# Gate and up products of a gated MLP as seven block products, with the order of work from a table

## The chip, the cores and the metric

The kernel runs on one core of one Trainium2 chip. The metric is the device time of one execution in microseconds (us); lower is better. A core has five engines that run side by side: TensorE (PE, the matrix engine; its weight loads are shown as PEld), VectorE (DVE), ScalarE (ACT), GpSimd (POOL) and SyncE (SP, which here only issues DMAs). Each engine works through its own queue in order and waits for the others through semaphores. SBUF is the working memory, PSUM the memory in which TensorE accumulates, in eight banks of 128 partitions x 512 float32.

## What is computed

Two layers over x of 2 x 1024 tokens with 256 channels: a mixture of gated MLPs, of which the two best of eight experts and one shared expert count for each batch row, and a linear layer with a LoRA mix.

```python
def mlp(x, gate_w, up_w, down_w):          # 256 -> 1024 -> 256
    g = einsum('bsh,hi->bsi', x, gate_w)
    u = einsum('bsh,hi->bsi', x, up_w)
    return einsum('bsi,ih->bsh', gelu(g, approximate=True) * u, down_w)

w, sel = top_k(softmax(cond), 2); w = w / w.sum()
x = x + sum(w_e * mlp(x, expert_e) for e in sel) + mlp(x, shared)
x = x + x @ W_base.T + b_base + 2 * lora(x, cond, As, Bs)
```

Everything is float32. The kernel splits each float32 operand v exactly into two parts, hi (v rounded to 12 significant bits, as float32r) and lo = v - hi, and forms a product as hi*hi + lo*hi + hi*lo: three matmuls for each float32 product.

## The kernel before

All is transposed: channels on the partitions, tokens on the free axis. A block is 512 tokens (T = 2 blocks for each of B = 2 batch rows), which is one PSUM bank. The 1024 hidden units of an expert are NI = 8 chunks of 128. `chunks` (L147 ff.) lists batch row, expert (s = 0 is the shared one) and chunk: 2 x 3 x 8 = 48 chunks. The main loop steps over chunks, and inside over the two token blocks: 96 steps.

A step (`gate_up`) forms the gate product g and the up product u. Each has two 128-row halves of the 256 channels, so each is 2 x 3 matmuls of 512 columns into one PSUM bank (`product`, L236). ScalarE applies gelu to g (L256), VectorE multiplies by u and, for an expert, by its weight (L259, L261), ScalarE makes the hi part (L263) and VectorE the lo part (L266). Two steps later (`DEPTH`) `down` multiplies these by the chunk's down weights, six matmuls (L282), which accumulate over all chunks of a batch row in the two banks of y of that block. So a step is 18 matmuls of 128x512.

Weights: a piece is two chunks, 768 KB. SP loads the shared ones; POOL gathers those of chosen experts by an indirect DMA (L169), with an index found by the router. Four raw buffers, loaded some seven chunks ahead. VectorE splits each chunk, 768 columns for gate, up and down together, in two instructions (L179, L183), which are put between a step's own instructions through the list `todo`.

At the start, 32 matmuls of constants run on PE while the first loads arrive; the first piece is loaded in column parts so that the first product can begin early. The LoRA matrix of a batch row (`weff_split`, `weff_mix`, `weff_add`) is made during the first chunks, in pieces spread over eight chunks of steps. The last layer (`lora`) of the first batch row runs inside the second row's first steps; at the end its stores are halved.

The order is that in which the Python code writes the instructions down: a last loop chains each engine's instructions in that order.

Of the kernel before, what the change touches and what calls it, by code (L numbers as in the profile page):

```python
"""x + top-2 mixture of gated MLPs with a shared expert, then + a linear layer with mixed LoRA.

Everything runs transposed: channels on partitions, tokens on the free axis, so that
no product needs a transpose on the chip. The host only permutes axes of the inputs.

One router row serves a whole batch row of 1024 tokens. The router runs on the chip; the
weights of the two chosen experts of each batch row are gathered by indirect DMAs with the
indices found there (the other experts enter the reference's sum with a weight of exactly 0).

The LoRA mix of a batch row is one matrix for all of its tokens, so  # L10
    W_eff[b] = W_base + 2 * sum_e cond[b, e] * Bs[e] @ As[e]
is formed once per batch row and the second layer is x + x @ W_eff[b].T + b_base.

Products: each float32 operand v is split exactly into float32r parts, hi = v rounded to 12
significant bits and lo = v - hi, which has at most 12. A product of two operands is then
three single-pass products, hi*hi + lo*hi + hi*lo, accumulated in float32; what lo*lo would
add is below half a unit in the last place of a float32 product.

Weights are outermost: each chunk of 128 hidden units is loaded and split once per batch row
and used for both of its token blocks.  # L20
"""
# [16 lines left out]
TB = 512      # tokens of a block: one PSUM bank of float32  # L38
TOP_K = 2
SCALING = 2.0  # LoRA's alpha / r  # L40
PIECE = 2     # chunks of 128 hidden units in one weight load
DEPTH = 2     # steps that a block's second product runs behind its first
WARM = 32     # products of constants that raise the tensor engine's clock while the first loads run
AHEAD = 3     # chunks that are split ahead of their use
LOAD_AHEAD = 7  # chunks that are loaded ahead of their use
# [3 lines left out]
def moe_then_lora(ctx: ExitStack, tc: tile.TileContext, xT, cond, skill, shared, wbT, bias,  # L49
# [5 lines left out]
    CW = 3 * C                      # weights of a chunk of 128 hidden units, per partition  # L55
    PW = PIECE * CW
    NPC = skill.shape[0] // (E * P)  # pieces of an expert
    NI = NPC * PIECE
    R = P // E
    S = NT // B  # L60
    T = S // TB

    const = ctx.enter_context(tc.tile_pool(name="const", bufs=1))
    rawp = ctx.enter_context(tc.tile_pool(name="rawp", bufs=4))
    wp = ctx.enter_context(tc.tile_pool(name="wp", bufs=7))
    xs = ctx.enter_context(tc.tile_pool(name="xs", bufs=4))
    xr = ctx.enter_context(tc.tile_pool(name="xr", bufs=2))
    work = ctx.enter_context(tc.tile_pool(name="work", bufs=4))
    resp = ctx.enter_context(tc.tile_pool(name="resp", bufs=4))
    post = ctx.enter_context(tc.tile_pool(name="post", bufs=2))  # L70
    ps_gu = ctx.enter_context(tc.tile_pool(name="ps_gu", bufs=2, space=bass.MemoryType.PSUM))
    ps_y = ctx.enter_context(tc.tile_pool(name="ps_y", bufs=2, space=bass.MemoryType.PSUM))

    def xview(n0):
        return xT[:, n0:n0 + TB].rearrange("(c p) n -> p c n", p=P)

    logits = const.tile([P, B, E], F32, name="logits")
    nc.gpsimd.dma_start(out=logits, in_=bass.AP(cond.tensor, 0, [[0, P], [E, B], [1, E]]))

# [1 line left out]
    row = const.tile([P, NPC], I32, name="row")  # L81
    nc.gpsimd.iota(row, pattern=[[1, NPC]], base=0, channel_multiplier=NPC)
    top = const.tile([P, B, 8], F32, name="top")
    gap = const.tile([P, B], F32, name="gap")
    ex = const.tile([P, B], F32, name="ex")
    sel = const.tile([P, B, 8], U32, name="sel")
    at = const.tile([P, B, TOP_K, NPC], I32, name="at")
    den = const.tile([P, B], F32, name="den")
    gate_w = const.tile([P, TOP_K, B], F32, name="gate_w")

    def router_max():
        for b in range(B):
            nc.vector.max(out=top[:, b, :], in_=logits[:, b, :])

    def router_exp():
        nc.vector.tensor_tensor(gap, top[:, :, 1], top[:, :, 0], ALU.subtract)
        nc.scalar.activation(ex, gap, AF.Exp)

    def router_index():
        for b in range(B):  # L100
            nc.vector.max_index(out=sel[:, b, :], in_max=top[:, b, :], in_values=logits[:, b, :])
        for b in range(B):
            nc.vector.scalar_tensor_tensor(
                at[:, b], sel[:, b, 0:TOP_K].unsqueeze(2).to_broadcast([P, TOP_K, NPC]), float(P * NPC),
                row.unsqueeze(1).to_broadcast([P, TOP_K, NPC]), ALU.mult, ALU.add,
            )

    def router_weights():
# [282 lines left out]
    while late:  # L391
        down(*late.pop(0))
# [59 lines left out]
```

## Time and profile before

| what | value |
|---|---|
| time, median of 3 runs | 420.66 us (420.38 to 420.96) |
| profiled execution, span on the core | 418.5 us, granted TensorE clock 0.995 |
| TensorE matmul busy | 411.1 us, 1832 instructions |
| VectorE / ScalarE / GpSimd busy | 226.4 / 126.3 / 25.5 us |
| 128x512 matmuls in the gate and up products / in the down products | 1152 / 576 |
| first matmul of the kernel's own / gapless from about | 5.2 us / 9.2 us |
| last result on VectorE ends / span ends | 415.0 / 418.5 us |

The span is the time from the first to the last instruction of one execution that the hardware profiler recorded. It is about 2 us below the median of the runs; sums are made against the span and then moved by this difference. "Busy" of PE is the union of overlapping matmuls; a group's row gives the length of one instruction from start to end, which is not the distance between two of them.

A line of a timeline has: start in us, duration in us, engine, source line, operation, output <- inputs, shapes, and in brackets the idle time before it with the one it waited for.

### The profile page before, as it was taken

What the parts mean: (1) busy time and instruction counts of PE and PEld (TensorE: products, weight loads), DVE (VectorE), ACT (ScalarE), POOL (GpSimd) and SP (SyncE); (2) the same over time, 40 slices, a digit from 0 to 9 for tenths busy, and PEclk for the clock granted to TensorE, in tenths of its full rate; (3) what the DMA queues carried; (4) which work ended last, traced back from release to release, by engine and by line L of the source; (5) the groups of instructions that cost most, each with busy time, mean ns of one, the idle gap of its engine ahead of it and who ended that gap; (6) DMA issues with size and microseconds to landing.
All of it is one profiled execution on the core that took longest, in us unless ns stands there. A gap on an engine that the chain in (4) does not pass through costs nothing.

```text
span 418.5 us, 4602 instructions
## 1 busy us (share of the span) xinstructions
PE 411.1 (98%) x1832; PEld 339.8 (81%) x1832; DVE 226.4 (54%) x351; ACT 126.3 (30%) x207; POOL 25.5 (6%) x27
## 2 busy tenths in 40 slices
PE   6999999999999999999999999999999999999996
PEld 5888888888888888888888888888888888888884
DVE  3956665454545445754695454544545454554346
ACT  3522223322222233222242222223322222333231
POOL 2201011011010000000030101001011000000000
PEclk8999999999999999999999999999999999999999
DMA  7752021120220322031027322022021000000003
GB/s 211 252 191 76 2 75 31 46 76 5 72 75 2 125 75 76 1 105 72 0 75 209 72 73 76 0 78 75 0 78 62 13 2 0 2 0 0 2 1 100
DMA packets 8837, 25.99 MB, mean 62 GB/s; under 512 B 1504, under 2 KB 2928, under 8 KB 8816
## 3 DMA queue, kind: packets, MB, share of 16 engines
q1 hardware_dynamic: 6480, 13.11, 9.7%
q0 software_dynamic: 2336, 12.59, 9.4%
q8 instruction: 14, 0.23, 0.2%
q14 instruction: 7, 0.06, 0.0%
HBM read 23.60 MB, written 2.10 MB: 61 GB/s over the span
## 4 chain that ended last, share of the span: by engine, by line
PE 95%; DMA 1%; DVE 1%; ACT 1%; issue 1%; SPq 0%; DVEq 0%
PE u L236 31%; PE g L236 31%; PE y L282 30%; PE o L236 2%; DMA x_raw<-in_xT 1%; ACT xa_hi L294 0%; PE wps L236 0%; DVE xa L293 0%; DVE xa_lo L297 0%; DVE act L261 0%; DVE x_lo L138 0%; ACT act_hi L263 0%; DVE res L311 0%; DVE x_hi L137 0%; SPq L152 0%
## 5 line engine op out<-in xcount | busy, mean ns | idle before, releaser
L261 DVE SCALAR_TENSOR_TENSOR act<-ge,gate_w,u 128x512 f32<-128x512 f32 x64 | 48.0, 749 | 118.7 <-PE u L236 118.5
L263 ACT CAST act_hi<-act 128x512 fp32r<-128x512 f32 x96 | 59.8, 622 | 146.4 <-DVE act L261 99.2
L256 ACT ACTIVATE ge<-g 128x512 f32<-128x512 f32 x96 | 57.5, 599 | 125.3 <-PE g L236 125.3
L236 PE MATMUL g<-x_hi,w_hi 128*128 128x512 f32 x192 | 75.0, 391 | 2.2 <-DVE x_hi L137 1.4
L236 PE MATMUL g<-x_lo,w_hi 128*128 128x512 f32 x192 | 75.1, 391 | 0.2 <-DVE x_lo L138 0.2
L236 PE MATMUL u<-x_hi,w_hi 128*128 128x512 f32 x192 | 75.2, 391 | 0.0
L236 PE MATMUL g<-x_hi,w_lo 128*128 128x512 f32 x192 | 75.0, 391 | 0.1
L236 PE MATMUL u<-x_lo,w_hi 128*128 128x512 f32 x192 | 75.1, 391 | 0.0
L236 PE MATMUL u<-x_hi,w_lo 128*128 128x512 f32 x192 | 74.9, 390 | 0.0
L266 DVE TENSOR_TENSOR act_lo<-act,act_hi 128x512 fp32r<-128x512 f32 x96 | 66.1, 688 | 12.7 <-ACT act_hi L263 12.5
L282 PE MATMUL y<-act_hi,w_hi 128*128 128x512 f32 x192 | 59.1, 389 | 0.0
L282 PE MATMUL y<-act_hi,w_lo 128*128 128x512 f32 x192 | 59.1, 389 | 0.0
L282 PE MATMUL y<-act_lo,w_hi 128*128 128x512 f32 x192 | 59.1, 389 | 0.0
L259 DVE TENSOR_TENSOR act<-ge,u 128x512 f32<-128x512 f32 x32 | 22.0, 687 | 46.9 <-PE u L236 46.8
L183 DVE TENSOR_TENSOR w_lo<-w_raw,w_hi 128x768 fp32r<-128x768 f32 x47 | 44.7, 951 | 0.0
L236 PEld LDWEIGHTS g<-x_hi,w_hi 128*128 128x128 f32 x192 | 36.1, 188 | 10.2 <-DVE x_hi L137 1.7
L236 PEld LDWEIGHTS g<-x_hi,w_lo 128*128 128x128 f32 x192 | 36.2, 189 | 7.9 <-POOL w_lo L159 0.5
L236 PEld LDWEIGHTS u<-x_hi,w_hi 128*128 128x128 f32 x192 | 36.3, 189 | 7.7
L236 PEld LDWEIGHTS g<-x_lo,w_hi 128*128 128x128 f32 x192 | 36.2, 188 | 7.8 <-DVE x_lo L138 0.5
L236 PEld LDWEIGHTS u<-x_lo,w_hi 128*128 128x128 f32 x192 | 36.3, 189 | 7.6
L236 PEld LDWEIGHTS u<-x_hi,w_lo 128*128 128x128 f32 x192 | 36.3, 189 | 7.6
L282 PEld LDWEIGHTS y<-act_hi,w_hi 128*128 128x128 f32 x192 | 36.0, 188 | 7.5
(53 smaller groups left out, 209.8 us busy)
## 6 DMA issues: line engine op xcount, KB each, us to landing
w_raw<-in_shared SPq DMA_DIRECT2D x7, 768.0 KB, 7.1
x_raw<-in_xT SPq DMA_DIRECT2D x8, 256.0 KB, 5.1
x_res<-in_xT SPq DMA_DIRECT2D x4, 512.0 KB, 5.6
outT<-res SPq DMA_DIRECT2D x6, 256.0 KB, 2.8
outT<-res SPq DMA_DIRECT2D x4, 128.0 KB, 2.5
w_raw<-in_shared SPq DMA_DIRECT2D x3, 128.0 KB, 4.7
w_raw<-in_shared SPq DMA_DIRECT2D x1, 384.0 KB, 6.7
wbT_sb<-in_wbT SPq DMA_DIRECT2D x1, 256.0 KB
```

What stands on the lines that cost most here:

```text
L183: nc.vector.tensor_tensor(lo, raw_w[j], hi.bitcast(F32), ALU.subtract)
L236: nc.tensor.matmul(ps, lhsT=l, rhs=r, start=(n == 0), stop=(n == len(parts) - 1))
L256: nc.scalar.activation(ge, g, AF.Gelu_apprx_tanh)
L259: nc.vector.tensor_tensor(act, ge, u, ALU.mult)
L261: nc.vector.scalar_tensor_tensor(act, ge, gate_w[:, s - 1, b:b + 1], u, ALU.mult, ALU.mult)
L263: nc.scalar.copy(hi, act)
L266: nc.vector.tensor_tensor(lo, act, hi.bitcast(F32), ALU.subtract)
L282: nc.tensor.matmul(y[:, c, :], lhsT=d[:, o:o + P], rhs=a, start=first and n == 0, stop=last and n == 2,)
```

## The change

The kernel is rewritten around a *group*: two chunks of hidden units and both token blocks of a batch row, for one expert. With 24 groups, gate (h = 0) and up (h = 1) of a group are each a product of a 2x2 block matrix (two chunks by two halves of the channels, A11 to A22) and a 2x2 block matrix of x (two halves of the channels by two token blocks). This is done by Strassen's scheme in Winograd's form: seven block products P1 to P7, of three matmuls each, instead of eight. For that,

- four sums of weight blocks are made on POOL for each group (`weight_sum`), of 128x256, gate and up side by side; and hi and lo parts of three plain blocks (`wa`, 128x768), four sums (`ws`, 128x1024) and the down weights (`wd`, 128x512);
- four sums of x blocks are made once for each batch row (`x_sum`), and hi and lo of seven operands instead of four;
- results are sums over several products. Some are accumulated in a PSUM bank: bank "a" of a half takes P1, then P6 on top, then P7, then P4; bank "d" takes P2, then P5 and P3. Between them ScalarE copies the partial sum of bank "a" to SBUF (`keep`, three for each half), and VectorE adds a kept part to bank "d" (`add_part`, three for each half).

Names: ij = (0,0), (1,1), (1,0), (0,1) are the four results of a group (chunk i, token block j). keep r1, u2 and u3 are the copies after P1, P6 and P7; add_part (0,0), (1,1), (0,1) are the sums with them, and (1,0) is what bank "a" holds after P4.

Every call is entered in a list with a time (`at(t, f, ...)`), a slot number: 22 slots for a group (`LEN`), each slot of PE being one block product or half a down product. The list is sorted by time and executed; each engine's queue follows from it. Tiles come from rings of fixed length (`Ring`): two raw weight buffers instead of four.

```diff
-WARM = 32     # products of constants that raise the tensor engine's clock while the first loads run
-AHEAD = 3     # chunks that are split ahead of their use
-LOAD_AHEAD = 7  # chunks that are loaded ahead of their use
+WARM = 32
+LEN = 22
...
+    raw_ring = Ring(sb, 2, [P, PW], F32, "w_raw")
+    wa_ring = Ring(sb, 2, [P, 2, 3 * G2], F32R, "wa")
+    sf = const([P, 4 * G2], F32, "sf")
+    ws_ring = Ring(sb, 2, [P, 2, 4 * G2], F32R, "ws")
+    bank = {(m, h): pp.tile([P, TB], F32, name=f"ps_{m}{'gu'[h]}", tag=f"{m}{h}")
+            for m in "ad" for h in (0, 1)}
...
+    def weight_sum(g, i, eng):
+        a, b, op = (
+            (raw_block(g, "A21"), raw_block(g, "A22"), ALU.add),
+            (ssum(0), raw_block(g, "A11"), ALU.subtract),
+            (raw_block(g, "A11"), raw_block(g, "A21"), ALU.subtract),
+            (raw_block(g, "A12"), ssum(1), ALU.subtract),
+        )[i]
+        eng.tensor_tensor(ssum(i), a, b, op)
...
+    def product(ps, terms, start=True):
+        parts = [p for (lh, ll), (rh, rl) in terms for p in ((lh, rh), (lh, rl), (ll, rh))]
+        for n, (l, r) in enumerate(parts):
+            nc.tensor.matmul(ps, lhsT=l, rhs=r, start=(start and n == 0), stop=(n == len(parts) - 1),
+                             skip_group_check=True)
...
+    def keep(m, h):
+        nc.scalar.copy(part[m, h], bank["a", h])
+
+    def add_part(g, h, ij, m):
+        sums[g, h, ij] = sum_ring[h].next()
+        nc.vector.tensor_tensor(sums[g, h, ij], bank["d", h], part[m, h], ALU.add)
...
+    for i in range(4):
+        at(-6.6 + i / 100, weight_sum, 0, i, G)
+    at(-6, split_ws, 0, hi_of, A)
+    at(-5.8, split_wa, 0, 2, 3, hi_of, A)
+    at(-5, x_sum, 0, 3, V)
+    at(-5, x_sum, 0, 1, V)
+    at(-5, x_sum, 0, 2, V)
+    at(-4.9, split_x, 0, "P6", hi_of, A)
+    at(-4.8, split_x, 0, "P6", lo_of, V)
+    at(-4.7, split_ws, 0, lo_of, V)
...
+    at(-3.9, split_x, 0, "P4", hi_of, A)
+    at(-3.8, split_x, 0, "P4", lo_of, V)
+    at(9.1, router)
+    at(-1, split_wd, 0, hi_of, A)
+    at(-0.9, split_wd, 0, lo_of, G)
+    for b in range(B):
+        at(7 + b, weff_split, b)
+        at(9.5 + b, weff_mix, b, y[b][0])
+        at(10.7 + b, weff_add, b, y[b][0])
+
+    ACT_AT = {(0, 0): 5.6, (1, 1): 15.6, (1, 0): 18.5, (0, 1): 21.5}
+    LO_AT = {(0, 0): 7.8, (1, 1): 18.0, (1, 0): 20.8, (0, 1): 23.5}
+    GE_AT = {(0, 0): 3.5, (1, 1): 14.4, (1, 0): 16.4, (0, 1): 18.4}
+    HI_AT = {(0, 0): 6.7, (1, 1): 16.8, (1, 0): 19.6, (0, 1): 22.6}
+    DOWN_AT = {(0, 0): (14, 19), (1, 1): (20, 21), (1, 0): (26, 31), (0, 1): (32, 35)}
+    PE_AT = (
+        (0, 0, "P1", "a", True), (1, 0, "P2", "d", True), (2, 1, "P1", "a", True), (3, 1, "P2", "d", True),
+        (5, 0, "P6", "a", False), (6, 0, "P5", "d", True), (7, 1, "P6", "a", False), (8, 1, "P5", "d", True),
+        (11, 0, "P7", "a", False), (12, 1, "P7", "a", False),
+        (15, 0, "P4", "a", False), (16, 0, "P3", "d", False),
+        (17, 1, "P4", "a", False), (18, 1, "P3", "d", False),
+    )
+    for g, (b, s, q) in enumerate(groups):
+        t0 = g * LEN
+        if g + 2 < NG:
+            at(t0 + 1.2, load_w, g + 2)
...
+        for t, m, h in ((1.3, "r1", 0), (3.3, "r1", 1), (6.3, "u2", 0), (8.3, "u2", 1),
+                        (12.3, "u3", 0), (13.3, "u3", 1)):
+            at(t0 + t, keep, m, h)
+        for t, h, ij, m in ((2.4, 0, (0, 0), "r1"), (4.4, 1, (0, 0), "r1"), (13.4, 0, (1, 1), "u3"),
+                            (14.3, 1, (1, 1), "u3"), (17.3, 0, (0, 1), "u2"), (19.5, 1, (0, 1), "u2")):
+            at(t0 + t, add_part, g, h, ij, m)
...
+        if g + 1 < NG:
+            n = g + 1
+            for i in range(4):
+                at(t0 + 1.5 + i, weight_sum, n, i, G)
+            at(t0 + 9.0, split_ws, n, hi_of, A)
+            at(t0 + 9.6, split_ws, n, lo_of, V)
+            at(t0 + 10.4, split_wa, n, 0, 3, hi_of, A)
+            at(t0 + 11, split_wa, n, 0, 3, lo_of, G)
+            at(t0 + 20.4, split_wd, n, hi_of, A)
+            at(t0 + 20.8, split_wd, n, lo_of, G)
```

In these calls A is ScalarE, V VectorE and G POOL. `weff_split`, `weff_mix`, `weff_add` and the whole router now stand in the first group (slots 7 to 11.7). For the second batch row, `x_sum` (POOL) and the splits of x are entered in groups 10 and 11, the residual adds `finish_y` of the first row in group 12, and the first row's last layer at the very end, between the last down products. There stores are of a whole 128x512 block.

## The prediction

> **What bounds the kernel now.** I read the page's busy time, then the chain that ended last, the groups, and timelines of start and middle.
>
> ```profile
> span 418.5 us, 4602 instructions
> ...
> PE 411.1 (98%) x1832; PEld 339.8 (81%) x1832; DVE 226.4 (54%) x351; ACT 126.3 (30%) x207; POOL 25.5 (6%) x27
> ...
> PE 95%; DMA 1%; DVE 1%; ACT 1%; issue 1%; SPq 0%; DVEq 0%
> ```
>
> TensorE (PE) is busy 98% of the span and is 95% of the chain; other engines end no wait that matters. Removing a matmul is worth its pitch, as long as the others keep up.
>
> ```profile
> L263 ACT CAST act_hi<-act 128x512 fp32r<-128x512 f32 x96 | 59.8, 622 | 146.4 <-DVE act L261 99.2
> L256 ACT ACTIVATE ge<-g 128x512 f32<-128x512 f32 x96 | 57.5, 599 | 125.3 <-PE g L236 125.3
> L236 PE MATMUL g<-x_hi,w_hi 128*128 128x512 f32 x192 | 75.0, 391 | 2.2 <-DVE x_hi L137 1.4
> ...
> L266 DVE TENSOR_TENSOR act_lo<-act,act_hi 128x512 fp32r<-128x512 f32 x96 | 66.1, 688 | 12.7 <-ACT act_hi L263 12.5
> ...
> L183 DVE TENSOR_TENSOR w_lo<-w_raw,w_hi 128x768 fp32r<-128x768 f32 x47 | 44.7, 951 | 0.0
> ```
>
> These durations price the new side work. Matmuls overlap: 391 ns is a latency; the chain shows six in 1.36 us, a pitch of 0.2267.
>
> ```profile
> 100.77 0.75 DVE L261 SCALAR_TENSOR_TENSOR act<-ge,gate_w,u 128x512 f32<-128x512 f32 x1 [1.95 <-PE u L236]
> ...
> 101.43 0.95 DVE L183 TENSOR_TENSOR w_lo<-w_raw,w_hi 128x768 fp32r<-128x768 f32 x1
> 101.55 0.62 ACT L263 CAST act_hi<-act 128x512 fp32r<-128x512 f32 x1 [1.56 <-DVE act L261]
> ...
> 102.30 0.68 DVE L266 TENSOR_TENSOR act_lo<-act,act_hi 128x512 fp32r<-128x512 f32 x1
> ```
>
> VectorE starts its next instruction 0.09 us before the last ends (0.66 for 0.75). So a 512-wide tensor_tensor occupies 0.60. At 17.00 and 17.53 two ScalarE instructions start 0.53 apart. An engine hands over to another in 0.03 to 0.06; a reader of PE starts 0.49 after the last matmul's start (398.11, then 398.60).
>
> ```profile
> 8.65 0.79 PE L236 MATMUL g<-x_lo,w_hi 128*128 128x512 f32 x1 [0.16 <-DVE x_lo L138]
> ...
> 10.37 0.75 POOL L159 TENSOR_TENSOR w_lo<-w_raw,w_hi 128x256 fp32r<-128x256 f32 x1 [1.07 <-ACT w_hi L158]
> ...
> 10.52 0.63 PE L236 MATMUL u<-x_hi,w_lo 128*128 128x512 f32 x1
> ...
> 10.56 1.10 DVE L138 TENSOR_TENSOR x_lo<-x_raw,x_hi 128x512 fp32r<-128x512 f32 x1
> ...
> 11.96 0.39 PE L236 MATMUL g<-x_hi,w_hi 128*128 128x512 f32 x1
> ```
>
> Two things of the start: x_lo beside a GpSimd (POOL) subtraction takes 1.10 instead of 0.69 and ends 0.54 after POOL does; and after PE's first waits the matmuls run at a pitch of 0.43 until 11.4. At 11.96, 12 matmuls (2.7 us) are done: the start costs 9.2.
>
> **The Trainium skill.** "SBUF — State Buffer", Who interferes with whom: a VectorE instruction with two SBUF inputs and a GpSimd instruction that reads SBUF exclude each other for their whole length. The x_lo above agrees. The indirect gather's POOL row (102.65, 1.22 us) beside act_lo at 0.68 shows no such effect. "TensorE: Matmul & The Clock Gate", What's actually happening: full clock returns after some 3.4 us of work; the slow pitch above agrees. "PSUM — Partial Sum Buffer" (The four PSUM rules) allows a synchronised read of a partial sum; no run here shows its price, so I price it as other PSUM reads.
>
> **Part 1, matmuls.** A group is two chunks and both token blocks. Before: 48 gate/up and 24 down matmuls. After: 14 block products of three, 42, and the same 24. 24 groups save 144 x 0.2267 = 32.6 us. PE's work was 391.7 (1728 matmuls) + 11.0 (last layer) + 1.4 (LoRA mix) = 404.1; it becomes 359.1 + 10.9 + 1.4 = 371.4. Every old matmul already loads its own weights at this pitch, so I leave the pitch.
>
> **Part 2, side work per group** (PE 66 x 0.2267 = 14.96 us). ScalarE: 15 instructions of 512 (six keeps, four gelus, four act_hi, one wd) x 0.53, a 1024 and a 768 (estimates from 405 ns at 256 and 622 at 512: 1.0 and 0.8): 9.8. VectorE: 13 to 14 of 512, x 0.60 to 0.66, and ws_lo of 1024, 1.14: 9.7. POOL: four sums at 0.73, lo of 768 (1.84, extrapolated) and of 512 (1.29): 6.1, plus 1.22 where it gathers. All fit singly. Sizes not in the trace: 1024 on VectorE is the 768 row plus one more step of 951 - 688 = 263 ns, 1.21 long; a ScalarE copy out of PSUM lies between gelu's 599 (from PSUM) and act_hi's 622 (a copy from SBUF), so nothing is gained or lost there; add_part is xa<-y,x_res again, 680 ns.
>
> Weight loads: the raw ring has two tiles instead of four. A load is issued behind POOL's last reading of the group before and is first read by the next weight sums, one group later. Landing took 7.1 us (shared) and 5.3 (gather), so about 8 us of cover is left; it costs nothing unless a transfer takes twice as long. The gather itself stands ahead of the four sums in POOL's queue: its 1.22 us is in the walk below.
>
> Order and latency: a slot is three matmuls, 0.68 us; slot k ends at 0.68(k+1), readers start 0.27 later. Walking one group in its queue orders without the lock: keep u3 g reads slot 11 at 8.43 and ends at 9.04 (P4 needs it at 10.14); add_part(1,1) g then ends at 9.76 (P3 needs it at 10.82); act_hi(1,1) ends at 12.30 (needed 13.54); times_up(0,1) ends at 15.82, act_hi(0,1) at 16.5, and keep r1 behind it in ScalarE's queue at 17.0, where the next P6 needs it at 18.3. Each is over 1 us early: PE stays the bound.
>
> With the lock, at two places: wd_lo becomes ready just as act_lo(1,0) ends and may go ahead of times_up(0,1), +1.1 us on the way to the next act_hi(0,1); and the four sums alternate with act_lo(0,1), times_up(0,0) and act_lo(0,0), so ws_hi, queued ahead of keep u3 on ScalarE, starts some 1 us later. Without POOL VectorE's loop (issue 12.0 plus waiting for ws_hi 0.9) closes in 12.9. Adding both places and wa_lo, POOL first each time, I get 15.4 in the 16 groups in which POOL also gathers, about 14.7 in the others. So 0 to 0.44 a group; I take 0.2 x 16 = 3.2.
>
> **Part 3, start.** Loads: the first four DMAs carry what the first ones did, so P1 and P2 finish at about 12.5 (slow pitch included). Then PE needs P6, whose bank waits for keep r1 g. On ScalarE that stands behind ws_hi, A22's hi, five x hi and wd_hi; on VectorE add_part stands behind three x sums, five x lo, ws_lo and a fourth sum. x11 lands at about 10.2 (before, its last x cast starts at 10.11); three x sums alternate with POOL's four sums: ws_hi at 13.3; P6 lo ends at 16.0, ws_lo at 17.2, three lo at 19.0, fourth sum 19.7, P4 hi 20.4, wd_hi 20.9, keep r1 at 21.4. Four slots are done then: PE idle for 9 us.
> Then VectorE carries the first group's extra work ahead of add_part(1,1): LoRA splits (2.0 + 1.2 us), router (1.6), ws_lo (1.1), two weff_add of three instructions (3.7; rows 683, 452, 693 ns), besides two adds, times_up, act_lo (2.5), a ScalarE table load for gelu (1.28; exp between two gelus adds two more of them behind this one, beside VectorE's router work) and 0 to 2 us of POOL's lock. That is 13.4 to 15.4: from 21.4 to about 35 or 37. P3 g starts 0.7 later, with 12 slots (8.2) and the mix (1.4) done: 26 to 28 lost. With the uncertain landings and P6's wait, 23 to 29; I take 26 (before 9.2). The router's gather index is needed only in group 2.
>
> **Part 4, batch change and tail.** Groups 10 to 12 add six x lo and four residual adds to VectorE (6.0 us), seven casts to ScalarE, and five 1.29 us instructions to POOL, of which two stand ahead of group 11's weight sums. Their slack is about 2 us a group: 1 to 6, I take 3. The tail stores 256 KB last instead of 128 KB; its VectorE order (finish_y, lo, store) leaves PE fed by the (0,1) second layer. 5.0 before, 4.6 to 5.2 after: 4.8.
>
> **Sum**: 371.4 + 26 + 3.2 + 3 + 4.8 = 408.4 against the profile's 418.5. The median shown, 420.66, is 2.2 above that span: 410.6, so 411.
>
> **Rivals.** A, this sum with its bounds: 402 to 421.
> B, the lock costs nothing: VectorE's instructions follow one another before POOL gets in, and the start takes 23. For: the walk's slacks of 1 us; against: the x_lo of 1.10. 371.4 + 23 + 0 + 1 + 4.8 = 400.2, time 402.
> C, slower: the lock becomes the loop. If every SBUF-reading POOL instruction holds up VectorE, its loop is 9.7 + 6.1 = 15.8 us a group, 0.8 over PE's: 23 x 0.8 = 18.4 in place of the 3.2, 423.6, time 426. It decides from (418.5 - 371.4 - 26 - 3 - 4.8)/23 = 0.58 us a group, a period of 15.5. For: VectorE works much of each group with two SBUF inputs; against: six adds read PSUM and are free of the lock, and half of POOL's work can fall beside them.
> D, the matmuls don't get fewer or take a longer pitch: the instruction order shows 42 and 24 a group. Under 0.02, counted in C.
>
> **How the numbers follow.** A 0.50, B 0.25, C 0.25. Forecast 411. The range 401 to 425 holds A, B and C's lower half. 0.2% (0.8 us) is what a measurement can tell from no change. Faster: A 0.46 + B 0.25 + C 0.03 = 0.74; same 0.02 + 0.02 = 0.04; slower 0.02 + 0.20 = 0.22.
>
> **What would show it.** The middle slices of the page: PE at 9 everywhere and a group each 14.96 us is B; 15.0 to 15.4 with waits of PE on keep, ws_hi's followers or add_part is A; 15.5 or more, with act_lo, times_up or ws_lo well over 0.69, 0.75 and 1.21, is C. The start: P6 at about 21 and P3 at 34 to 38 is right; P3 before 30 makes me wrong by that much. If PSUM reads between products take much over 0.62, or the pitch leaves 0.2267, Parts 1 and 2 fall.

## The result, and the profile after

| | before | after |
|---|---|---|
| median of the runs | 420.52 us (420.28 to 420.96) | 416.45 us (415.53 to 416.95) |
| ratio of the times, 95% interval | | 0.9893 (0.9875 to 0.9911) |
| span of the profiled execution | 418.5 us | 414.7 us |

The change makes the kernel 4.1 us faster; 9.7 us were forecast. The page of the changed kernel shows, in the lines that answer to those shown of before (span; busy time of each engine; in tenths, the busy share of PE in 40 slices of the span, and the clock granted to it; the chain that ended last):

```profile
span 414.7 us, 4765 instructions
...
PE 388.6 (94%) x1676; PEld 312.5 (75%) x1676; DVE 330.6 (80%) x425; ACT 260.0 (63%) x435; POOL 207.5 (50%) x177
...
PE   7287999999999999999889999999999999999993
...
PEclk8678999999999999999999999999999999999998
...
PE 68%; DVE 11%; issue 8%; POOL 5%; ACT 4%; DMA 3%; SPq 1%; DVEq 0%; POOLq 0%
```

PE is busy for 22.5 us less, but it was busy 98% of the span and is now busy 94%; only 68% of the chain are its own, where it was 95%. The slices say where: the first four (a slice is 10.4 us) read 7287, and the 20th and 21st read 88, in the middle of the span, where one batch row follows the other. Between these two places and behind the second PE is full (90% or more in each slice). The groups show what the others paid (instructions of one kind; busy us, mean ns of one, then idle time before them):

```profile
L151 DVE TENSOR_TENSOR acts<-act,acts 128x512 fp32r<-128x512 f32 x96 | 78.4, 816 | 34.1 <-ACT acts L148 31.6
...
L279 DVE SCALAR_TENSOR_TENSOR act<-ge,gate_w,c_u 128x512 f32<-128x512 f32 x48 | 58.4, 1217 | 4.0 <-DVE c_u L264 0.5
L190 POOL TENSOR_TENSOR sf<-w_raw 128x256 f32<-128x256 f32 x48 | 51.8, 1080 | 1.5 <-DMA w_raw<-in_shared 1.0
```

times_up with both inputs in SBUF takes 1217 ns where it took 749 with one of them in PSUM, act_lo 816 instead of 688. The form alone is not the reason, since the same times_up takes 739 ns at its shortest, where no POOL instruction runs beside it: the exclusion between VectorE and POOL is there. In an ordinary group it costs next to nothing, as the next view shows. Its rows are whole groups, each from the start of its P1 to that of the next (us; then busy us and number of instructions of PE, PEld, DVE, ACT and POOL, granted clock, DMA share, GB/s): group 2, then groups 10, 11, 12 and 13.

```profile
55.37:70.33 14.96, 14.96 (x67) 12.33 (x66) 12.09 (x16) 10.25 (x17) 8.40 (x8) 1.00 0.18 54
175.55:191.02 15.47, 15.25 (x68) 12.31 (x66) 13.06 (x17) 10.37 (x18) 9.04 (x7) 1.00 0.14 52
191.02:209.97 18.95, 16.50 (x68) 11.93 (x66) 17.32 (x20) 12.31 (x23) 12.47 (x10) 1.00 0.11 42
209.97:227.12 17.15, 15.81 (x68) 12.15 (x66) 14.76 (x20) 10.56 (x18) 8.49 (x7) 1.00 0.31 108
227.12:243.41 16.29, 15.55 (x68) 12.23 (x67) 12.82 (x18) 10.92 (x19) 7.21 (x7) 1.00 0.33 113
```

A group without side work of the second row takes 14.96 to 15.07 us (group 22 alone 15.48), where 66 matmuls at 0.2267 are 14.96; before, 72 took 16.32. Groups 10 to 13 take 0.5, 4.0, 2.2 and 1.3 us more, 8.0 in all. So the span adds up as 371.4 (PE's work) + 26.8 (start) + 1.6 (groups 1 to 9 and 14 to 22, of which 0.5 in group 22) + 8.0 (groups 10 to 13) + 7.0 (tail) = 414.8, the span but for rounding. The start's 26.8 is where group 1 begins, 40.40, less the 12.24 of the 18 slots done by then and the 1.4 of the LoRA mix; the tail's 7.0 is the span less the start of group 23 (379.12), one group (14.96) and the 13.6 of work that then remains (four half down products, 2.7, and the last layer, 10.9).

Where group 11 loses its 4.0 us is seen in its timeline (start, duration, engine, line, output <- inputs; in brackets the idle time before it and whom it waited for):

```profile
193.08 1.75 POOL L224 TENSOR_TENSOR xr<-xr,xr 128x512 f32<-128x512 f32 x1
...
194.87 0.96 PE L247 MATMUL ps_ag<-x,ws 128*128 128x512 f32 x3 [0.29 <-ACT r_g L258]
194.91 1.62 POOL L226 TENSOR_TENSOR xr<-xr,xr 128x512 f32<-128x512 f32 x1
...
196.03 0.97 PE L247 MATMUL ps_dg<-x,ws 128*128 128x512 f32 x3 [0.19 <-DVE c_g L264]
...
199.49 1.18 POOL L190 TENSOR_TENSOR sf<-w_raw,sf 128x256 f32<-128x256 f32 x1
200.70 1.05 ACT L148 CAST ws<-sf 128x1024 fp32r<-128x1024 f32 x1 [1.26 <-POOL sf L190]
...
203.53 0.96 PE L247 MATMUL ps_ag<-x,wa 128*128 128x512 f32 x3 [1.08 <-ACT u_g L258]
...
206.53 0.98 PE L247 MATMUL ps_du<-x,ws 128*128 128x512 f32 x3 [0.61 <-DVE c_u L264]
...
208.47 1.66 PE L301 MATMUL y<-acts,wd 128*128 128x512 f32 x6 [0.28 <-ACT acts L148]
```

Two sums of x (L224, L226) stand ahead of the four weight sums in POOL's queue; the last weight sum ends at 200.67, 9.65 us after the group's start (in group 10 it ended 5.1 after). ws_hi waits for it on ScalarE, and keep u3 g stands behind ws_hi, so P4 waits 1.08. One thing about reading such waits: the number in brackets counts from the *end* of the last matmul, so it leaves out 0.39 - 0.23 = 0.16 us of pipeline that drains, and the three matmuls after a wait show 0.96 where three without one show 0.84. Each wait costs the bracket and some 0.28 more. The five add up to 2.45 + 5 x 0.28 = 3.85, against 3.99 measured: all but 0.14 of the group's loss is these five waits.

P4's wait is 1.4 of the 8.0 us that groups 10 to 13 lose. The larger part comes at P6 and P5, which wait for keep r1 g and add_part(0,0) g. Group 12, in PE's timeline:

```profile
214.43 0.96 PE L247 MATMUL ps_ag<-x,ws 128*128 128x512 f32 x3 [0.89 <-ACT r_g L258]
215.83 0.96 PE L247 MATMUL ps_dg<-x,ws 128*128 128x512 f32 x3 [0.44 <-DVE c_g L264]
```

Group 13 has 0.29 and 0.45 at the same two products, group 11 the 0.29 and 0.19 above, group 10 only 0.22 at P5. With 0.28 more for each, these seven waits are 4.7 of the 8.0 us.

The start (PE's timeline): P6 at 19.50, P3 g at 34.57, with the slow pitch behind it.

```profile
19.50 1.65 PE L247 MATMUL ps_ag<-x,ws 128*128 128x512 f32 x3 [7.81 <-ACT r_g L258]
...
34.57 1.04 PE L247 MATMUL ps_dg<-x,ws 128*128 128x512 f32 x3 [2.81 <-DVE c_g L264]
35.41 1.48 PE L247 MATMUL ps_au<-x,wa 128*128 128x512 f32 x3
36.69 1.48 PE L247 MATMUL ps_du<-x,ws 128*128 128x512 f32 x3
```

Three matmuls in 1.28 (35.41 to 36.69) are a pitch of 0.43, half speed: the idle time ahead of P3 was followed by some 2.5 us at half the clock, about 1.8 us lost in all until the pitch was back at 38. The tail (VectorE's timeline, the last four results of the kernel):

```profile
405.63 0.74 DVE L379 SCALAR_TENSOR_TENSOR res<-ps_ag,bias_sb,xa 128x512 f32<-128x512 f32 x1
407.70 0.75 DVE L379 SCALAR_TENSOR_TENSOR res<-ps_au,bias_sb,xa 128x512 f32<-128x512 f32 x1 [1.33 <-DMA outT<-res]
408.95 0.75 DVE L379 SCALAR_TENSOR_TENSOR res<-ps_dg,bias_sb,xa 128x512 f32<-128x512 f32 x1 [0.50 <-DMA outT<-res]
410.01 0.75 DVE L379 SCALAR_TENSOR_TENSOR res<-ps_du,bias_sb,xa 128x512 f32<-128x512 f32 x1 [0.30 <-DMA outT<-res]
```

Six results come at the end and there are three tiles for them (`res_ring`), so the last three wait for the stores of the first three.

### The profile page after: what moved, and what is told of

Read it like the earlier page. It is cut to its first block, busy times and chain, and to the rows that moved or that the text cites. A ratio compares the mean times of both kernels' runs of the same rounds, so it can differ in the third digit from the quotient of the medians.

```text
span 414.7 us, 4765 instructions
## 1 busy us (share of the span) xinstructions
PE 388.6 (94%) x1676; PEld 312.5 (75%) x1676; DVE 330.6 (80%) x425; ACT 260.0 (63%) x435; POOL 207.5 (50%) x177
## 4 chain that ended last, share of the span: by engine, by line
PE 68%; DVE 11%; issue 8%; POOL 5%; ACT 4%; DMA 3%; SPq 1%; DVEq 0%; POOLq 0%
PE y L301 25%; PE ps_au L247 12%; PE ps_ag L247 12%; PE ps_dg L247 10%; PE ps_du L247 9%; DVE act L279 2%; POOL sf L190 2%; DMA w_raw<-in_shared 2%; ACT acts L148 2%; DVE acts L151 2%; DVE c_g L264 1%; POOL wd L151 1%; DVE act L277 1%; DVE x L151 1%; DVE res L379 1%
## 5 line engine op out<-in xcount | busy, mean ns | idle before, releaser
L301 PE MATMUL y<-acts,wd 128*128 128x512 f32 x576 | 147.1, 390 | 1.1 <-DVE wef L344 0.8
L301 PEld LDWEIGHTS y<-acts,wd 128*128 128x128 f32 x576 | 108.3, 188 | 24.9 <-DVE wef L344 1.2
L148 ACT CAST acts<-act 128x512 fp32r<-128x512 f32 x96 | 59.5, 620 | 77.2 <-DVE act L279 53.2
L151 DVE TENSOR_TENSOR acts<-act,acts 128x512 fp32r<-128x512 f32 x96 | 78.4, 816 | 34.1 <-ACT acts L148 31.6
L151 POOL TENSOR_TENSOR wa<-w_raw,wa 128x768 fp32r<-128x768 f32 (+1 forms) x26 | 53.1, 2041 | 64.4 <-ACT wa L148 64.4
L271 ACT ACTIVATE ge<-c_g 128x512 f32<-128x512 f32 x72 | 45.6, 634 | 27.2 <-DVE c_g L264 26.1
L279 DVE SCALAR_TENSOR_TENSOR act<-ge,gate_w,c_u 128x512 f32<-128x512 f32 x48 | 58.4, 1217 | 4.0 <-DVE c_u L264 0.5
L190 POOL TENSOR_TENSOR sf<-w_raw 128x256 f32<-128x256 f32 x48 | 51.8, 1080 | 1.5 <-DMA w_raw<-in_shared 1.0
L247 PE MATMUL ps_dg<-x,ws 128*128 128x512 f32 x144 | 42.7, 405 | 4.3 <-DVE c_g L264 4.3
L247 PE MATMUL ps_du<-x,ws 128*128 128x512 f32 x144 | 42.0, 401 | 0.6 <-DVE c_u L264 0.6
```

What stands on the lines that cost most here:

```text
L148: (eng.copy if eng is nc.scalar else eng.tensor_copy)(pair[:, 0, :], src)
L151: eng.tensor_tensor(pair[:, 1, :], src, pair[:, 0, :].bitcast(F32), ALU.subtract)
L190: eng.tensor_tensor(ssum(i), a, b, op)
L247: nc.tensor.matmul(ps, lhsT=l, rhs=r, start=(start and n == 0), stop=(n == len(parts) - 1), skip_group_check=True)
L271: nc.scalar.activation(ge[g, ij], result(g, 0, ij), AF.Gelu_apprx_tanh)
L279: nc.vector.scalar_tensor_tensor(act[g, ij], ge[g, ij], gate_w[:, s - 1, b:b + 1], result(g, 1, ij), ALU.mult, ALU.mult)
```

## The experiments

All times are medians; ratios are to the kernel before, on the same chip. A group's length is read here from its P2 to the next group's P2, within 0.02 of the P1 to P1 above. The start's length differs from one profile to the next: where it was left as it is, P2 of group 2 began between 55.00 and 56.57, so a difference of span under some 1.5 us says little by itself, and the groups' lengths are compared.

### The sums of x earlier

The sums of x are spread over groups 7, 8 and 9, with the loads and P1's split ahead of them.

```diff
-            at(t0 - 18 + n / 10, load_x, b, k, j)
+            at(t0 - 4 * LEN - 18 + n / 10, load_x, b, k, j)
...
-        at(t0 + 12, x_sum, b, 3, G)
-        at(t0 + 22, x_sum, b, 1, G)
-        at(t0 + 23, x_sum, b, 2, G)
+            early = 3 * LEN * (1 - n)
+            at(t0 - early + 9 + n, split_x, b, p, hi_of, A)
+            at(t0 - early + 10 + n, split_x, b, p, lo_of, V)
+        at(t0 - 3 * LEN + 6, x_sum, b, 3, G)
+        at(t0 - 2 * LEN + 6, x_sum, b, 1, G)
+        at(t0 - 1 * LEN + 6, x_sum, b, 2, G)
```

> Edit: the second batch row's x is loaded in group 5, P1's operand split in group 7 and the three x sums 3, 1, 2 made on GpSimd in groups 7, 8 and 9, one each, behind the weight sums; all else stays. Theory 1 (in group 11 two x sums stand ahead of the weight sums in GpSimd's queue, so ws_hi is late and blocks the keeps behind it on ScalarE): the period of group 11 falls from 18.95 us to about 16.5 and the groups behind it recover sooner, span 409 to 411 instead of 414.7. Rival (VectorE's six extra lo parts and four residual adds are the cost, GpSimd's order is not): group 11 stays above 18, span 413.5 to 415.

Measured: 415.64 us, ratio 0.9889 (0.9872 to 0.9906), span 413.1. Group 11 fell from 18.95 to 17.06 (its wait for P4 is gone), but group 7, which now holds P1's split and a sum, rose to 16.63 and group 8 to 15.50; groups 12 and 13 kept 17.14 and 16.29. What group 11 gained was paid elsewhere: groups 2 to 22 together are only 0.5 us shorter. The other 1.05 us of span lie in the start, which this edit doesn't touch (P2 of group 2 begins at 55.00 here, at 56.05 in the changed kernel). Neither expectation held in full: group 11 came between the two, and the span gained less than the theory had. So the sums ahead of the weight sums were the cause of group 11's longest wait, and moving them is not yet a gain: what counts is what they stand beside.

### Eight result tiles

```diff
+    store_tiles = [*res_ring.tiles, *ge_ring.tiles, part["u3", 0], part["u3", 1]]
...
-        r = res_ring.next()
+        r = store_tiles.pop(0)
```

> Edit: the eight stores at the end each have a tile of their own (three of the result ring, and gelu and kept-part tiles that are no longer in use) instead of three tiles in turn. Theory (three of the last results wait for the DMA of the store three before, 1.33, 0.50 and 0.30 us): the last result starts at about 408.3 instead of 410.0, span 413.0. Rival (the final stores share the DMA engines and land at the same time whenever they are issued): span 414.5 to 415.

Measured: 414.21 us, ratio 0.9843 (0.9827 to 0.986), span 412.5: 2.2 less. The last result starts at 407.70 instead of 410.01, and waits for PE (0.59), no longer for a store. Of the 2.2 us, 0.6 lie ahead of group 23, which begins at 378.55 instead of 379.12; the tail itself is 1.6 shorter, 5.4 instead of 7.0, and it is 5.4 in each of the three later versions with eight tiles. So most of the tail's excess over the forecast is the three tiles; the last 0.6 was not traced.

### A lighter start

The router goes forward, and the hi and lo of the LoRA weights, needed only at the end, go to the last group.

```diff
-        hi_of(lora["W", b], f, nc.vector)
-        lo_of(lora["W", b], f, nc.vector)
...
-    at(9.1, router)
+    at(-6.69, router)
...
+        at((NG - 1) * LEN + 2.2 + 2 * b, weff_hi_lo, b, hi_of, A)
+        at((NG - 1) * LEN + 2.3 + 2 * b, weff_hi_lo, b, lo_of, G)
```

> Edit: the router's work stands in front of the first weight sums' casts, where VectorE waits for x, and hi and lo of the two LoRA matrices move from VectorE in group 0 to ScalarE and GpSimd in the last group. Theory (amount of VectorE work ahead of add_part(1,1) sets the start): 4.4 us less of it there, so P3 of group 0 starts at about 30.2 instead of 34.6, its wait is too short for the clock to fall, and the span falls by 4.4 to 6.2. Rival (the late start of P6 sets it): P3 within 1 us of 34.6.

Measured: 414.64 us, ratio 0.9848 (0.9815 to 0.9881), span 412.7. P3 g came at 34.01, where the theory had 30.2 and the rival "within 1 us of 34.6"; but it came at full clock, so that group 1's P2 began at 38.80 instead of 41.09. What took the place of the work removed (VectorE's timeline; on POOL wa_lo ran from 26.37 for 1.93):

```profile
26.68 1.77 DVE L148 CAST lora_B<-sbf 128x256 fp32r<-128x256 f32 x1
```

A cast of 128x256 that takes 0.29 us in the changed kernel stood still until POOL's wa_lo was over, and the LoRA mix, which needs it, started at 28.51 after a wait of 1.81. Then PE's clock fell (three matmuls in 1.28, from 30.63 to 31.91):

```profile
30.63 1.48 PE L247 MATMUL ps_au<-x,ws 128*128 128x512 f32 x3
31.91 1.48 PE L301 MATMUL y<-acts,wd 128*128 128x512 f32 x3
```

So P3 no longer waited for VectorE, whose add_part(1,1) g was over at 32.17, and not for P6 either: it came when PE had got through the products ahead of it. The rival's number was met without its cause. "SBUF — State Buffer", Who interferes with whom, in the Trainium skill says that casts too can take the pair of ports that VectorE shares with GpSimd, and that the one which comes second stands still for the whole instruction; 1.77 for 0.29 agrees.

### Keep r1 forward in the first group

P1 and P2 of group 0, their keeps and add_parts, ahead of the splits of x.

```diff
-            at(t0 + t, block_product, g, h, p, ps, start)
+            at(t0 + t if g or t > 3 else -6.66 + t / 100, block_product, g, h, p, ps, start)
...
-            at(t0 + t, keep, m, h)
+            at(t0 + t if g or m != "r1" else -6.5 + h / 10, keep, m, h)
...
-            at(t0 + t, add_part, g, h, ij, m)
+            at(t0 + t if g or m != "r1" else (-6.3, -4.85)[h], add_part, g, h, ij, m)
```

> Edit: in group 0 alone, keep r1 and add_part(0,0) stand in their queues right behind the first operand splits instead of behind all of them. Theory (after P6 the start is set by VectorE's and GpSimd's work and by the lock between them, not by P6's start): P6 starts at about 15.5 instead of 19.5, P3 of group 0 at 33 to 34 instead of 34.6, span 413 to 414.7. Rival (the 8 us in which PE waits for P6 are the loss): P3 at about 30.5 and span near 410.5.

Measured: 415.36 us, ratio 0.9881 (0.9864 to 0.9897), span 413.7. PE's timeline:

```profile
14.14 1.52 PE L247 MATMUL ps_ag<-x,ws 128*128 128x512 f32 x2 [2.77 <-ACT x L148]
...
34.69 0.98 PE L247 MATMUL ps_dg<-x,ws 128*128 128x512 f32 x3 [2.30 <-DVE c_g L264]
35.51 0.86 PE L247 MATMUL ps_au<-x,wa 128*128 128x512 f32 x3
```

P6 is 5.4 us earlier and P3 is not earlier at all (34.57 before): the idle time only moved. P6's wait of 7.81 us, the longest one shown above, costs nothing, because VectorE's work ahead of add_part(1,1) decides when P3 comes. The clock this time stayed full after a wait of 2.30, so that group 1 began at 38.95 instead of 40.40; group 1 then took 0.8 more. What is left of the gain is inside the spread of the start.

### Instructions added, and where

To price a further instruction on VectorE or POOL, sums that nobody reads were added to the changed kernel, into a tile of their own: two on VectorE in group 4 at slots 10 and 11, ahead of add_part(1,1); two on POOL in group 7 ahead of the weight sums; four on VectorE in group 16.

```diff
+    at(4 * LEN + 10, extra, V, 4)
+    at(4 * LEN + 11, extra, V, 4)
+    at(7 * LEN + 1.4, extra, G, 7)
+    at(7 * LEN + 1.45, extra, G, 7)
+    at(16 * LEN + 10, extra, V, 16)
...
+    at(16 * LEN + 10.3, extra, V, 16)
```

> Edit: additions that nothing uses: two VectorE instructions of 128x512 with two SBUF inputs in group 4 (slots 10, 11), four in group 16 (slot 10), two GpSimd ones ahead of the weight sums in group 7. Theory (the loop has well under 1 us to spare a group): groups 4 and 5 together 0.5 to 1.2 us longer than the 30.0 without them, groups 16 to 18 together 1.5 to 2.5 longer, groups 7 and 8 together 1.5 to 3.5 longer. Rival (2 us of slack a group, as the prediction had it): 0, at most 0.6 and at most 1.0.

Measured in a single run: 427.44 us beside 420.67. Group 4 took 18.74 (3.75 more; groups 4 and 5 together 3.7), groups 7 and 8 together 2.3 more, group 16 19.73 (4.75 more). The prediction's 2 us of slack is refuted, but the theory's own prices for the VectorE pairs, 0.5 to 1.2 and 1.5 to 2.5, were far too low as well. VectorE, on which two such sums occupy 1.2 us:

```profile
95.07 3.06 DVE L215 TENSOR_TENSOR scratch<-x 128x512 f32<-128x512 f32 x2
98.05 0.68 DVE L273 TENSOR_TENSOR c_g<-ps_dg,u_g 128x512 f32<-128x512 f32 x1
```

and PE:

```profile
98.79 1.48 PE L256 MATMUL ps_dg<-x,ws 128*128 128x512 f32 x3 [1.86 <-DVE c_g L273]
100.07 1.48 PE L256 MATMUL ps_au<-x,wa 128*128 128x512 f32 x3
```

wa_lo had started on POOL at 94.70 and ran for 2.15; the two sums have both inputs in SBUF and stood behind it, and add_part(1,1) g stood behind them. It reads PSUM and could have run beside wa_lo: in the changed kernel a sum of the LoRA mix with one input in PSUM (29.35) took 0.68 while wa_lo ran from 28.38 to 31.12. The wait costs 2.1, and half clock over the next three slots the rest.

The same two instructions at other places:

```diff
+    at(4 * LEN + 10, extra_psum, 4)
+    at(4 * LEN + 11, extra_psum, 4)
+    at(7 * LEN + 8.5, extra, V, 7)
+    at(7 * LEN + 8.6, extra, V, 7)
+    at(16 * LEN + 19.6, extra, V, 16)
+    at(16 * LEN + 19.7, extra, V, 16)
```

> Edit: two added VectorE instructions of 128x512 in each of three groups, which nothing uses: in group 4 at slots 10 and 11 as in the first probe, but reading PSUM and one SBUF operand; in group 7 with two SBUF operands at slot 8.5, ahead of ws_lo; in group 16 with two SBUF operands at slot 19.6, behind add_part(0,1). Theory (what cost 3.75 us in the first probe was the lock: two SBUF operands queued ahead of add_part while wa_lo runs on GpSimd, and then PE's slow clock after a wait of 1.9 us): group 4 at most 0.8 us longer, group 7 at most 0.8, group 16 at most 0.8. Rival (VectorE's loop is simply full: any two instructions cost over 1.2 us): each of the three 1.2 us or more, in its group and the next.

Measured in a single run: 418.67 us beside 420.76. With one input in PSUM, at the slots of the first probe, the pair costs groups 4 and 5 together 0.97 instead of 3.7; with two SBUF inputs at slot 8.5, ahead of wa_lo, 0.38; at slot 19.6, ahead of the results for the next group, 1.26. The theory had at most 0.8 for each: the first is a little above it, and the third is as dear as the rival had said of all three. One pair of instructions, 1.2 us long, costs from 0.4 to 3.7: there is no slack "of a group" that it could be held against, there are places.

### The second row's work, placed by these prices

Splits at slot 8.5, one sum of x in each of groups 7 to 10 at slot 6, behind the weight sums; the fourth sum takes the place of x10 instead of x11, so that P3's operand is split in group 12.

```diff
-    moving = {"P1": (0, 0), "P2": (1, 0), "P3": (1, 1), "P5": (0, 0), "P6": (0, 1), "P7": "T3", "P4": (1, 1)}
+    moving = {"P1": (0, 0), "P2": (1, 0), "P3": (1, 1), "P5": (0, 0), "P6": (0, 1), "P7": "T3", "P4": (1, 0)}
...
+        at(t0 - 4 * LEN + 8.5, split_x, b, "P1", lo_of, V)
...
+        at(t0 - 3 * LEN + 8.5, split_x, b, "P2", lo_of, V)
+        for n, i in enumerate((3, 1, 2, 4)):
+            at(t0 + (n - 3) * LEN + 6, x_sum, b, i, G)
...
+        at(t0 + 2 * LEN + 8.5, split_x, b, "P3", lo_of, V)
...
-                at(t0 + (10.2, 14.2)[t] + c / 10, finish_y, b, t, c)
+                at(t0 + (9.5, 17.4)[t] + c / 100, finish_y, b, t, c)
```

In this version the load of a residual block of row 0 takes the tile of x11 before P3's split has read it: P3 of the second row is computed with that block, so the version does not compute that row as the layer has it, and only its times are of use.

> Edit: for the second batch row, the loads of x go to group 4, the four x sums one each behind the weight sums of groups 7 to 10 (the fourth in the place of x10), the lo parts of P1 and P2 to slot 8.5 of groups 6 and 7, those of P6, P5 and P7 to slot 8.5 of group 11 and that of P3 to slot 8.5 of group 12, where GpSimd is idle; the residual adds move to slots 9.5 and 17.4. As much work as before on every engine. Theory (the 8.0 us that groups 10 to 13 take beyond 15.0 each come from where these instructions stand: ahead of the weight sums, or ahead of add_part while wa_lo holds the lock): groups 6 to 13 together lose at most 3.5, span 409.5 to 411. Rival (the amount of VectorE work is the cost): they lose 6.5 to 8, span 413 to 415.

Measured: 417.84 us, ratio 0.9935 (0.9916 to 0.9954), span 415.8. Group 11 falls to 15.82, but group 7 (P2's split and a sum) takes 16.62, and group 12 takes 20.41: P3's split on VectorE waits 2.66 us for that load, everything behind it waits too, and PE for the residual add. Groups 6 to 13 lose 10 us together, where the theory had 3.5 at most and the rival 6.5 to 8. A place that is right for the engine was wrong for the tile.

The same with the start and the tail mended (the lighter start, keep r1 forward, the LoRA splits forward, eight result tiles) and the same block of the second row:

> Edit: the eight store tiles, the light start (router early, hi and lo of the LoRA matrices late), keep r1 and add_part first in group 0, the boundary of the run before this one, and both LoRA splits ahead of times_up(0,0) of group 0. Theory: tail 2.2 us, boundary 4 us and start 4 to 6 us shorter: span 402 to 405, time 404 to 407. Rival (the gains are not additive, since the start stays bound by the lock and the slow clock): span 406 to 410.

Measured: 413.14 us, ratio 0.9837 (0.9817 to 0.9856), span 410.5. Group 1's P2 begins at 36.66 (41.09 in the changed kernel) and the tail is as with eight tiles; groups 7, 8, 11, 12 and 13 lose 9.5 us, among them 4.4 in group 12, with the same wait; so the span stayed above both expectations. Start and tail can be had independently of the boundary.

### One instruction of the second row in a group

Loads in group 2, P1's and P2's splits in groups 4 and 5, sums in 6 to 9, and the two residual loads that took the tile behind P3's split.

```diff
+            at(t0 - 8 * LEN + 4 + n / 10, load_x, b, k, j)
...
+        at(t0 - 6 * LEN + 8.5, split_x, b, "P1", lo_of, V)
...
+        at(t0 - 5 * LEN + 8.5, split_x, b, "P2", lo_of, V)
+        for n, i in enumerate((3, 1, 2, 4)):
+            at(t0 + (n - 4) * LEN + 6, x_sum, b, i, G)
...
+        at(t0 + 2 * LEN + 3.6, split_x, b, "P3", hi_of, A)
+        at(t0 + 2 * LEN + 6, split_x, b, "P3", lo_of, G)
...
-                at(t0 + 4 - 12 * (b == B - 1) + t + c / 10, load_res, b, t, c)
+                at(t0 + 4 - 12 * (b == B - 1) + 2.3 * t + c / 10, load_res, b, t, c)
```

> The second row's preparation is thinned out: its loads in group 2, the splits of P1 and P2 in groups 4 and 5, one sum of x in each of groups 6 to 9 (the fourth now written over the tile of x10, so that it need not wait for the row's end), the splits of P6, P5, P7 and P4 in group 11, of P3 in group 12 (its low half on GpSimd), and the two residual loads of tokens 512 on issued behind P3's split, so that nothing is overwritten. Theory 1 (instructions of the second row cost nothing by themselves; what costs is two of them in one group, or one ahead of what the next group waits for): groups 4 to 9 and 11 at most 15.5 us each, group 12 at most 16.5, groups 4 to 13 together at most 3.5 us above ten times 14.97, span 410 to 411.5, time about 412. Rival (each such instruction costs about its own share of its engine wherever it is put): groups 4 to 9 each 15.5 or more, and the span no better than 413.5.

Measured: 412.44 us, ratio 0.9799 (0.978 to 0.9819), span 410.7. Groups 4 to 13: 14.96, 15.45, 15.03, 15.05, 15.05, 15.05, 15.52, 15.48, 16.26, 16.57, together 4.7 us above ten times 14.97, where 3.5 at most was expected and the changed kernel has 8.4. A sum of x of 1.3 us on POOL costs nothing that can be told in such a place: groups 6 to 9 take 15.03 to 15.05, and 15.02 to 15.07 in the changed kernel, which has none there. P2's split costs group 5 0.4, P1's split group 4 nothing. Groups 12 and 13 still lose 1.3 and 1.6, all of it at P6 and P5, whose waits are for keep r1 g and add_part(0,0) g.

With start and tail mended too:

> The former plus the lighter start, the kept parts of the first group forward, the LoRA splits forward, and eight result tiles. If the three gains add: start -4.0 (group 1 begins near 36.7), boundary -4.5 to -6, tail -2: span 403 to 405.5, time 404.5 to 407, below the 411 that was forecast for the change. If the boundary's loss only moves: span 409 to 411.

Measured: 407.31 us, ratio 0.9684 (0.9668 to 0.97), span 406.1, slightly over what was expected: groups 1, 5 and 22 still lose about 0.5 each, which had not been counted.

### Keep r1 ahead of the last result

What is left at P6 goes over one way that the prediction had walked: wd_lo on POOL holds up times_up(0,1), which holds up act_hi(0,1), behind which keep r1 g of the next group stands on ScalarE. Nobody needs act_hi(0,1) soon, so it and its lo go behind:

```diff
-    LO_AT = {(0, 0): 7.8, (1, 1): 18.0, (1, 0): 20.8, (0, 1): 23.5}
+    LO_AT = {(0, 0): 7.8, (1, 1): 18.0, (1, 0): 20.8, (0, 1): 24.41}
...
-    HI_AT = {(0, 0): 6.7, (1, 1): 16.8, (1, 0): 19.6, (0, 1): 22.6}
+    HI_AT = {(0, 0): 6.7, (1, 1): 16.8, (1, 0): 19.6, (0, 1): 23.32}
```

> The changed kernel with one order altered in every group: the last of a group's four results, act_hi(0,1) and act_lo(0,1), stand behind keep r1 g on ScalarE and behind add_part(0,0) g on VectorE of the next group, instead of ahead of them; its down product is ten slots away. Theory 1 (what is left of the lock reaches TensorE on one way: wd_lo on GpSimd holds up times_up(0,1), which holds up act_hi(0,1), behind which keep r1 g stands, for which P6 waits): the waits of P6 and P5 at the start of groups 10 to 13 go, groups 10, 12 and 13 come to 15.2 or less, group 11 loses about 1 us of its 4 (it keeps the late weight sums), the steady groups stay at 14.96 to 15.05; span 410 to 411.5, time about 412.5. Rival (the second row's work is too much for VectorE in these groups, and the wait turns up at another product): groups 12 and 13 stay above 15.8, span 413.5 or more.

Measured: 413.49 us, ratio 0.9824 (0.9807 to 0.9842), span 412.7. Every group from 1 to 9 and from 14 to 22 takes 14.96, and group 13 too (16.29 before): the lock's share in the loop is gone, and with it these 1.6 + 1.3 us. But group 11 took 19.59 and group 12 16.97, and the start 0.9 us more. PE:

```profile
204.22 0.96 PE L247 MATMUL ps_ag<-x,wa 128*128 128x512 f32 x3 [2.40 <-ACT u_g L258]
...
221.71 1.32 PE L301 MATMUL y<-acts,wd 128*128 128x512 f32 x3 [0.79 <-DVE xa L357]
```

With P6 no longer late, PE reaches the late weight sums sooner and waits 2.40 there instead of 1.08; and in group 12 a down product now waits for a residual add that had time enough as long as P6 held PE up. For groups 11 and 12 the rival was right: the wait turned up at another product.

Both together, with start and tail:

> The kernel with the lighter start, the spread second row and the eight result tiles, plus that order. Theory 1: the 0.5 + 0.5 + 1.3 + 1.6 us that groups 10 to 13 still lose go down to 0.8 at most: span 402.5 to 404, time 404 to 405.5. Rival: span 405.5 or more.

Measured: 401.82 us, ratio 0.9551 (0.9535 to 0.9567), span 399.9: 18.8 us faster than before, and below what was expected. The page:

```profile
PE 384.8 (96%) x1676; PEld 314.7 (79%) x1676; DVE 338.1 (85%) x420; ACT 261.2 (65%) x435; POOL 214.2 (54%) x180
...
PE   7669999999999999999999999999999999999995
...
PE 91%; DVE 5%; DMA 1%; ACT 1%; issue 0%; SPq 0%; DVEq 0%
```

and the place of the lock, in POOL's, VectorE's and ScalarE's timelines at the end of a group:

```profile
170.84 1.29 POOL L151 TENSOR_TENSOR wd<-w_raw,wd 128x512 fp32r<-128x512 f32 x1 [3.84 <-ACT wd L148]
```

```profile
170.88 1.80 DVE L279 SCALAR_TENSOR_TENSOR act<-ge,gate_w,c_u 128x512 f32<-128x512 f32 x1
```

```profile
171.57 0.59 ACT L258 COPY r_g<-ps_ag 128x512 f32<-128x512 f32 x1 [0.81 <-PE ps_ag L247]
172.71 0.62 ACT L148 CAST acts<-act 128x512 fp32r<-128x512 f32 x1 [0.55 <-DVE act L279]
```

times_up still takes 1.80 behind wd_lo, VectorE is busier than in the changed kernel (85%), and PE waits for neither: r_g now waits for PE, and the cast that waits for times_up has a slot of its own behind it. All groups take 14.95 to 14.97, but 12 and 13 with 15.45 and 15.25. Against the version before this one that is 6.2 us: groups 10 to 13 give 3.1, the other groups 2.5 and the start 0.5. The two versions differ in that order alone.

## Why the prediction was right and wrong

The direction held, for the reason given; the gain was less than half of the 9.7 us. Term by term of its sum, in us of span:

| term | forecast | measured |
|---|---|---|
| PE's work (Part 1) | 371.4 | 371.4: 66 matmuls a group, period 14.96 |
| start (Part 3) | 26 | 26.8 |
| loop, lock (Part 2) | 3.2 | 1.6, of which 0.5 in group 22 |
| batch change (Part 4) | 3 | 8.0 |
| tail (Part 4) | 4.8 | 7.0 |
| sum | 408.4 | 414.8 (span 414.7) |

*Part 4 failed.* The step was "Their slack is about 2 us a group: 1 to 6, I take 3"; 8.0 were measured, outside its own range. It compared six lo's, four adds and five POOL instructions with the time that an engine is idle in a group. That idle time is there (VectorE is busy 12.1 of 14.96), but it is not one sum: the probes show 1.2 us of VectorE's work costing 0.4 to 3.7 by its place. The prediction even held the fact that makes group 11 the worst, "of which two stand ahead of group 11's weight sums", and did not walk it through: two sums of x, 3.4 us, then four weight sums, then ws_hi and wa_hi on ScalarE, then keep u3, then P4, which is due 10.1 after the group's start. With the last sum ending at 9.65 instead of 5.1 and three ScalarE instructions behind it, P4 must be late. The walk that Part 2 had made for an ordinary group, made again for group 11, would have shown it. That way cost 1.4 us at P4. The dearer one, 4.7 us at P6 and P5, is the other end of the same walk: keep r1 g and add_part(0,0) g stand behind the last result of the group before, and the more than 1 us by which they came early in an ordinary group was used up in groups 10 to 13. With those two put ahead, and the second row's work spread, 0.8 of the 8.0 us is left. Which of the second row's instructions used up the cover in which group was not taken apart. The batch change also reaches one group further than "Groups 10 to 12": group 13 starts late for the same keep r1 and loses 1.3.

*The tail* counted work and the size of the last store, and missed a buffer: six results, three tiles. Eight tiles gave 1.6 of the 2.2 us back.

*Part 2* named the place of the lock rightly: "wd_lo becomes ready just as act_lo(1,0) ends and may go ahead of times_up(0,1), +1.1 us": times_up takes 1.79 for 0.75 in nearly every group, 1.04 more. It cost 0.11 a group at most, but for 0.5 in group 22, since keep r1 had more than 1 us of cover, as the walk said; where that cover is used up (groups 10 to 13) the waits behind it cost 0.5 to 1.9 us. Rival B was near in its price and wrong in its reason: POOL does get in between VectorE's instructions. Rival C, the lock as the loop, fell: VectorE's sum of waits fits into the period even at 85% busy.

*Part 3* came within 1 us, partly by luck. "P6 at about 21 and P3 at 34 to 38" was said; they came at 19.50 and 34.57. The half clock after the wait, 1.8 us, was not in it, and made up for VectorE being early. That VectorE's queue and not P6's wait sets the start was the prediction's reading, and the version with P6 at 14.14 bears it out.

*The rest*: PSUM reads between two products changed nothing in PE's pitch (ScalarE's keeps 0.58, the pitch 0.2267), and the span stood 1.75 below the median instead of 2.2. In every execution recorded the time is 1.7 to 1.9 above the span; the 2.2 had set the median of three runs against the span of another, faster one.

## What to carry to other kernels

When side work is added to a loop that one engine bounds, don't hold its length against the idle time of its engine: walk the queue, and ask of each new instruction what stands behind it and when that is due. An instruction that is needed late belongs behind those that the bound engine needs next, even if it is ready first; with that order alone the lock between VectorE and GpSimd cost the ordinary groups nothing here, though it held VectorE up as before. And count buffers as well as engines wherever work that used to be spread comes in one burst.

## What the hardware showed that was not expected

Once the start's longest waits were over, TensorE's clock fell to half after rather short waits, and not after every one. After waits of 1.67, 1.81, 1.86, 2.81 and 2.99 us, and of 2.83 in five runs, the pitch went to 0.43, at once or some 2 us later, and stayed there for 2 to 4 us. After 2.30 and 2.40 it did not, nor after 2.83 and 2.84 in two other runs, nor after another wait of 1.67; after 1.3 or less it never did. "TensorE: Matmul & The Clock Gate", What's actually happening, in the Trainium skill puts the fall at an idle window of about 3.4 us, and says that the windows run on their own, whatever the kernel does. Windows of their own would fit that waits of 2.83 and of 1.67 did it in one run and not in another, but the runs here show falls after half of such a window. As an estimate from the 1.8 us lost behind P3 in the changed kernel, a wait of over 1.6 us on the way of the bound engine should be priced with up to 1.8 us more.
